# Keys spread by transfers into kept tiles, attention outputs in even rows, and another order of the transfers, in a four-layer conditioned transformer kernel

## The chip, the cores and the metric

The kernel runs on one core of one Trainium2 chip. The metric is the device time of one execution in microseconds. The kernel before was run three times: 1624.05, 1625.13 and 1627.65 us, median 1625.13 us. All arithmetic is float32. In what follows the engines are called PE (matrix multiply; PEld is its weight load), DVE (vector), ACT (activation), POOL (general purpose) and SP (here it only issues transfers); SPq is SP's queue of transfers.

## The reference: what is computed

The input x holds 128 sequences of 64 tokens with 128 channels; there is one conditioning vector for each sequence, and a context of 64 tokens for each. Four layers follow each other, all with residual connections:

- Layer 0: self-attention (normalised x, scaled and shifted by the condition; a gate from the condition on the result), cross-attention to the context, and a gated MLP of 512 hidden units.
- Layer 1: cross-attention to the normalised and modulated context.
- Layer 2: self-attention, cross-attention and MLP like layer 0, with weights of its own.
- Layer 3: attention to the context as a prototype bank, then three routed experts and a gate.

The change touches the attentions of layers 0 to 2, which all have 16 heads of 8 channels:

```python
q = _heads(xn @ q_w + q_b)                       # 16 heads of 8 channels
k, v = (context or xn) @ kv_w + kv_b
attn = softmax(einsum('bhnd,bhsd->bhns', q, k) * SCALE)
o = einsum('bhns,bhsd->bhnd', attn, v)           # back to 128 channels
x = x + gate * (o @ proj_w + proj_b)             # no gate in the cross-attentions
```

## The kernel before

**Tiling and stages.** The 8192 tokens are cut into 16 groups of 512 (8 sequences of 64), and x stays in SBUF in 16 tiles. The program goes through the stages one after the other, each over 16 groups: L0s (self-attention of layer 0), L0c (cross-attention), the MLP of layer 0, L1c, L2s, L2c, the MLP of layer 2, and layer 3. Together the five attention stages are 80 groups.

**Order of the work.** The order on every engine is written out by hand: the program runs under a manual schedule, and each engine takes its instructions in the order of the calls. `attend` is a software pipeline. Its `step(k)` handles a half group (k = 2i + u): the scores of half k, the first half of the exponentials of half k-1, the weighted sums of half k-2, and pieces of two generators, `prepare` for groups up to four ahead and `finish` for groups one to three behind. All transfers are issued by SP in the order of the calls, too. Eight completion semaphores (lanes) are used in turn, so a transfer that is issued waits for the one eight places before it.

**A half group** (`scores`, `turned`, `weighted`): 32 small matmuls give the scores `sc` in PSUM (line 478; the tile has one buffer), DVE takes the maximum `mx` (line 485) and writes the difference `e` (line 487), PE transposes it to `pp` (line 503), ACT takes the exponential `eT` (line 507), PE multiplies it with the values, `po` (line 520), and ACT copies that to `o` (line 528). The weights of the last product, `vbd`, hold the values of a pair of heads and, in two columns, ones, so that the sums of the exponentials (the denominators) come out as further rows of `o`. There are two such tiles, kept for the whole of the attentions; their zeros and ones are written once.

**Keys.** One matmul takes four heads at a time over 32 rows. So the keys of a group, `kT` (line 438, 128 channels by 512 tokens), are spread into `kbd`, which has four copies of it; copy j keeps only the channels of head j of each four, and the rest is zero. Before, POOL makes the four copies by multiplying with a column of 0 and 1 in `mask` (line 444); in the first group of layer 0 DVE does it:

```python
for j in range(4):
    (V if at.get("first") else G).tensor_scalar(
        kbd[:, j], by_batch(kT), mask[:, j : j + 1], 1.0, ALU.mult, ALU.mult
    )
```

**The end of a group** (`finish`, in four pieces). First piece: two transfers bring the rows of denominators of `o` to `sums` in DRAM (line 538), one brings them back as `rc` on 128 partitions (line 542), and four move the odd head pairs' rows of `o` beside the even ones (line 545). Second piece: DVE takes the reciprocal (line 547), a transfer stores it as `recs` (line 549), in the self stages two transfers load the gates `gt` from their table in DRAM (line 278), and one loads the reciprocals back, each repeated over the eight rows of its head, as `rb` (line 554). Third piece: POOL multiplies `o` by `rb` to `oT` (line 557) and adds the bias to x (line 559). Fourth piece: PE projects `oT`, `py` (line 563), and DVE (and in the self stages POOL) adds the result to x (lines 565 to 569).

**The start.** `condition` transposes the condition and the rows of biases; DVE then takes the statistics of the first x tile (line 313), POOL the inverse deviation (lines 329 and 330), DVE normalises (line 372), PE transposes (line 342), DVE modulates (line 357), and PE makes the first keys (line 436).

Of the kernel before, what the change touches and what calls it, by code (L numbers as in the profile page):

```python
# [9 lines left out]
F32 = mybir.dt.float32  # L10
AF = mybir.ActivationFunctionType
ALU = mybir.AluOpType
# [23 lines left out]
for _name, _n in _VECS:  # L36
# [13 lines left out]
    "L3_xcond_router_W": (3, 3), "L3_xcond_e_w1": (9, 256), "L3_xcond_e_w2": (6, 128),  # L50
    "L3_xcond_gate_w1": (3, 128), "L3_xcond_gate_w2": (1, 128), "L3_xcond_out_w": (1, 128),
}
_RAW = [
    "x", "cond_1024", "ctx_1024", *_WTS,
    "L0_xcond_ca_proj_b", "L1_xcond_bp", "L2_xcond_b_cproj", "L3_xcond_router_b", "L3_xcond_e_b2",
# [4 lines left out]
def tile_kernel(ctx: ExitStack, tc: tile.TileContext, a: dict, out: bass.AP):  # L60
# [5 lines left out]
    def const(shape, name):  # L66
        return cp.tile(shape, F32, tag=name, name=name)
# [8 lines left out]
    nc.sync.dma_start(cond, a["cond_1024"])  # L76
    vec_rows = const([_NVEC, P], "vec_rows")
    nc.scalar.dma_start(vec_rows, a["vecs"])
    mask = const([P, 4], "mask")
    nc.scalar.dma_start(mask, a["mask"])  # L80

    w = {}

    def load_weights(prefix, pool=cp):
        for name, (k, n) in _WTS.items():
            if name.startswith(prefix):
                t = pool.tile([P, k, n], F32, tag=name, name=name)
                src = a[name]
                if len(src.shape) == 3:
                    src = src.rearrange("e c n -> (e c) n")  # L90
                nc.sync.dma_start(t, src.rearrange("(k p) n -> p k n", p=P))
                w[name] = t

    xs = [const([P, TT, P], f"x{s}") for s in range(NST)]
# [23 lines left out]

    ident = const([P, P], "ident")
    make_identity(nc, ident)  # L120
    nhalf = const([P, TT], "nhalf")
    G.memset(nhalf, -0.5)

# [37 lines left out]
    def mm(name):  # L161
        return pools[1].tile([P, 512], F32, tag="mm", name=name)
# [4 lines left out]
        Places.ak.tile([P, NB, 8, 32], F32, tag=f"vbd{i}", name=f"vbd{i}", bufs=1) for i in range(2)  # L167
    ]

    def clear(t):  # L170
        G.memset(t, 0.0)
        G.memset(t[0:L, :, :, 16:17], 1.0)
        G.memset(t[L:P, :, :, 17:18], 1.0)


# [2 lines left out]
    condT = const([P, P], "condT")  # L178
    scT = const([P, P], "scT")
    mods = {}  # L180

    def col(name, i=0):
        r = _ROW[name] + i
        return vec[:, r : r + 1]
# [19 lines left out]

    def folded_column(wp, bp, bv, i):
        pb = mm("pb")
        T.matmul(pb[:, 0:1], w[wp][:, 0], col(bv, i), start=True, stop=True)
        t = const([P, 1], "pb_" + wp)
        V.tensor_add(t, pb[:, 0:1], col(bp))
        proj_bias[wp] = t  # L210
# [3 lines left out]
    def gate_table(wmod, wp, i=2, bias=None):  # L214

        table = dp.tile([P, 2, P], F32, tag="gate_" + wp, name="gate_" + wp)
        rows = const([P, 2, P], "gate_rows")
        gb = const([P, P], "gate_bias")
        V.tensor_scalar_mul(gb, mods[wmod][:, i, :], proj_bias[wp] if bias is None else bias)

        def second():
            pg = mm("pg")
            for q, src in enumerate((mods[wmod][:, i, :], gb)):
                T.transpose(pg[:, ts(q, P)], src, ident)
            V.tensor_copy(rows, pg[:, 0 : 2 * P].rearrange("p (i c) -> p i c", i=2))
            nc.sync.dma_start(table, rows)
            gates[wp] = table

        return second

    def folded_row(wp, bp, bv):
        bvs = const([P, P], "bvs")
        V.tensor_copy(bvs, col(bv, 1).broadcast_to([P, P]))

        def second():
            pb = mm("pb")
            T.matmul(pb[:, :P], bvs, w[wp][:, 0], start=True, stop=True)
            V.tensor_add(row_bias[bp], row_bias[bp], pb[:, :P])
            proj_bias[wp] = row_bias[bp]

        return second

    def condition():
        pc = mm("pc")
        T.transpose(pc[:, :P], cond, ident)
        V.tensor_copy(condT, pc[:, :P])
        S.activation(scT, pc[:, :P], AF.Silu)
        pv = mm("pv")
        T.transpose(pv[:, :_NVEC], vec_rows, ident[:_NVEC, :_NVEC])
        V.tensor_copy(vec, pv[:, :_NVEC])  # L250
        V.tensor_scalar_add(vec1, vec, 1.0)

    first_mods = modulations("L0_xcond_adaln_w", "L0_xcond_adaln_b", 6, (1, 4))
# [19 lines left out]
    def gate_tile(pool, s, wp):  # L273

        gt = pool.tile([P, TT, 2, P], F32, tag="gt", name="gt")
        for h in range(2):
            r = gates[wp].rearrange("(s t h) i c -> s h t (i c)", t=TT, h=2)[s, h]
            nc.sync.dma_start(
                gt[ts(h, L)].rearrange("p t i c -> p t (i c)"),
                r.unsqueeze(0).broadcast_to([L, TT, 2 * P]),  # L280
            )
        return gt

# [15 lines left out]
    def by_batch(t):  # L299
        return t.rearrange("p (b l) -> p b l", b=NB)  # L300
# [80 lines left out]

    turn = [0]

    ctxT = dp.tile([NST, P, NT], F32, tag="ctxT", name="ctxT")

    def prepare(pools, at):
# [52 lines left out]
        i = turn[0] % 2  # L439
        turn[0] += 1  # L440
        vbd = vbds[i]
        kbd = pool.tile([P, 4, NB, L], F32, tag="kbd", name="kbd")
        for j in range(4):
            (V if at.get("first") else G).tensor_scalar(  # L444
                kbd[:, j], by_batch(kT), mask[:, j : j + 1], 1.0, ALU.mult, ALU.mult
            )
        yield
        pq = psum.tile([P, 512], F32, tag="mm", name="pq")
        T.matmul(pq, at["wq"], q_in, start=True, stop=True)  # L449
# [11 lines left out]
                    start=True, stop=True,  # L461
                )
        pv4 = pvv.rearrange("p b (i d) -> p b i d", d=HD)
        S.copy(vbd[0:L, :, :, 0:HD], pv4[0:L])
        S.copy(vbd[L:P, :, :, HD : 2 * HD], pv4[L:P])
        at["vbd"] = vbd

    def scores(pools, at, u):
# [61 lines left out]
    def finish(pools, at):  # L530

        pool, psum = pools[:2]
        s, o = at["s"], at["o"]
        cross = at["layer"][2] == "c"

        sums = dp.tile([16, NT], F32, tag="sums", name="sums", bufs=2)
        for j in range(2):
            nc.sync.dma_start(
                sums.rearrange("(g i j) t -> j g i t", i=2, j=2)[j], o[16 + j : P : 32, :, :]
            )  # L540
        rc = pool.tile([P, L], F32, tag="rc", name="rc")
        nc.sync.dma_start(rc, sums.rearrange("h (c t) -> (h c) t", t=L))

        for g in range(4):
            nc.sync.dma_start(o[32 * g + 16 : 32 * g + 32, 0, :], o[32 * g : 32 * g + 16, 1, :])
        yield
        V.reciprocal(rc, rc)
        recs = dp.tile([16, NT], F32, tag="recs", name="recs", bufs=2)
        nc.sync.dma_start(recs.rearrange("h (c t) -> (h c) t", t=L), rc)

        if not cross:
            gt = gate_tile(pool, s, at["wp"])
        rb = pool.tile([P, NT], F32, tag="rb", name="rb", bufs=1)
        nc.sync.dma_start(rb, recs.unsqueeze(1).broadcast_to([16, HD, NT]))
        yield
        oT = pool.tile([P, NT], F32, tag="oT", name="oT", bufs=1)
        G.tensor_tensor(oT, o[:, 0, :], rb, ALU.mult)  # L557
        bias = proj_bias[at["wp"]].unsqueeze(1).broadcast_to([P, TT, P]) if cross else gt[:, :, 1, :]
        G.tensor_tensor(xs[s], xs[s], bias, ALU.add)
        yield  # L560
        py = psum.tile([P, TT, P], F32, tag="mm", name="py")
        for t in range(TT):
            T.matmul(py[:, t, :], oT[:, ts(t, P)], w[at["wp"]][:, 0], start=True, stop=True)  # L563
        if cross:
            V.tensor_add(xs[s], xs[s], py)
        else:
            y = pool.tile([P, TT, P], F32, tag="y", name="y")
            V.tensor_tensor(y, py, gt[:, :, 0, :], ALU.mult)
            G.tensor_tensor(xs[s], xs[s], y, ALU.add)

    def attend(pools, ats):
# [5 lines left out]
        def go(gens, i):  # L577
            if 0 <= i < n:
                next(gens[i], None)
# [8 lines left out]
        def step(k, between=(), late=()):  # L588
# [11 lines left out]
            if past:  # L600
                weighted(pools, past["at"], past["u"], past["eT"])
            if u == 0:
                go(fin, i - 2)
                go(prep, i + 4)
                go(prep, i + 1)
                go(fin, i - 3)
            else:
                go(prep, i + 1)
# [16 lines left out]
    def attention_of(s, layer):  # L625
        if layer[2] == "s":
            wmod, wqkv, bqkv, wp = {
                "L0s": ("L0_xcond_adaln_w", "L0_xcond_qkv_w", "L0_xcond_qkv_b", "L0_xcond_sa_proj_w"),
                "L2s": ("L2_xcond_W_mod", "L2_xcond_W_qkv", "L2_xcond_b_qkv", "L2_xcond_W_proj"),
            }[layer]  # L630
            m = w[wqkv][:, 0]
            return dict(
                s=s, layer=layer, wmod=wmod, wp=wp, wq=m[:, 0:P], bq=col(bqkv, 0),
                wk=m[:, P : 2 * P], bk=col(bqkv, 1), wv=m[:, 2 * P : 3 * P],
            )
        wq, bq, wkv, bkv, wp = {
            "L0c": (
# [8 lines left out]
        }[layer]  # L646
        m = w[wkv][:, 0]
        return dict(
            s=s, layer=layer, wp=wp, wq=w[wq][:, 0], bq=col(bq), wk=m[:, 0:P], bk=col(bkv, 0),
            wv=m[:, P : 2 * P],  # L650
        )

# [537 lines left out]
    def stages():  # L1190
# [41 lines left out]
        clear(vbds[0])  # L1232
        ahead_1(0, 1, 2, 3)
        condition()
        ahead_1(0, 0)
        first_mods[0]()
        ahead_1(0, 0, 1, 2, 0, 0, 1)
# [11 lines left out]
            f()  # L1249
        first_mods[2]()  # L1250
        n = last + 2 + len(heads_0)
        for f in steps_1[6:-n]:
            f()
        for s in range(2):
            heads_0[3 + s] = lambda s=s, f=heads_0[3 + s]: (f(), load_context(s))
        rest = into_mlp(steps_1, heads_0, turns_0)
# [68 lines left out]
```

## Time and profile before

| | |
|---|---|
| runs | 1624.05, 1625.13, 1627.65 us |
| profiled execution | 1626.31 us, span 1624.5 us |
| PE busy | 1573.8 us (97%) |
| DVE busy | 1240.4 us (76%) |
| ACT busy | 1035.5 us (64%) |
| POOL busy | 1072.5 us (66%) |
| `kbd` on POOL | 316 instructions, 212.4 us |
| L0s, first to last start of a group | 16.94 to 204.38 us |
| L0c | 210.47 to 397.72 us |
| L1c | 544.51 to 733.13 us |
| L2s | 739.11 to 925.19 us |
| L2c | 931.28 to 1118.47 us |

The span is one execution as the hardware profiler recorded it; the profiled execution's own time includes what lies around the span. Each attention stage is read at its starts of `mx` for the even halves: a group takes 11.9 to 12.3 us in the steady part. The MLPs and layer 3 fill the time between and after. A "released by" entry in a group of instructions names what ended the idle time before them.

### The profile page before, as it was taken

Reading aid. Unit: us, or ns where it says so; the run is one execution under the profiler, and the core shown is the slowest. Engines: PE = TensorE matmul, PEld = TensorE weight load, DVE = VectorE, ACT = ScalarE, POOL = GpSimd, SP = SyncE. Lnnn points to the kernel's source line nnn. Section 1 sums busy time; section 2 is a strip of 40 time slices with the busy share of each in tenths; the row PEclk is TensorE's granted clock in tenths of the full one; section 3 lists DMA queues with packets and bytes.
Section 4 is the critical chain, followed back from the end, with each engine's and each line's share of the span. In section 5 each row is a group of like instructions: output and inputs, shape, how many; then the busy total and the mean of one; then the engine's idle time right before and its main releaser. Section 6 shows DMA issues by size and latency. Waiting matters only on the chain.

```text
span 1624.5 us, 64028 instructions
## 1 busy us (share of the span) xinstructions
PE 1573.8 (97%) x27842; PEld 1086.8 (67%) x27842; DVE 1240.4 (76%) x1566; ACT 1035.5 (64%) x1710; POOL 1072.5 (66%) x1786
## 2 busy tenths in 40 slices
PE   6999999998999899999999999998999999999998
PEld 4676777776544577776777777776777566666665
DVE  7898998898555688899899889896443566666666
ACT  5788777776433678878888888886334544444443
POOL 6687787766888789887787876775875333333322
PEclk9999999999999999999999999999999999999999
DMA  8334453332111022211334432222533111111100
GB/s 209 85 82 99 107 127 92 83 83 72 55 36 55 16 63 61 72 44 50 90 82 102 104 88 73 62 56 59 130 81 76 31 39 37 40 33 36 34 12 19
DMA packets 146775, 112.65 MB, mean 69 GB/s; under 512 B 36357, under 2 KB 125247, under 8 KB 146495
## 3 DMA queue, kind: packets, MB, share of 16 engines
q1 hardware_dynamic: 146288, 108.53, 26.1%
q8 instruction: 219, 3.59, 0.9%
q14 instruction: 61, 0.50, 0.1%
q10 hardware_dynamic: 207, 0.03, 0.0%
HBM read 83.99 MB, written 14.02 MB: 60 GB/s over the span
## 4 chain that ended last, share of the span: by engine, by line
PE 83%; DVE 12%; ACT 3%; issue 1%; DMA 0%; SPq 0%; DVEq 0%
PE sc L478 10%; PE pp L503 9%; PE po L520 7%; PE ph L693 7%; PE ph L1080 6%; PE ph L1081 6%; DVE e L487 6%; DVE mx L485 6%; PE po L1111 5%; PE psT L342 5%; PE pk L436 5%; PE py L563 4%; PE py L709 4%; PE py L699 3%; PE pvv L459 3%; PE pq L449 3%
## 5 line engine op out<-in xcount | busy, mean ns | idle before, releaser
L507 ACT ACTIVATE eT<-pp 128x1024 f32<-128x1024 f32 x320 | 329.7, 1030 | 160.8 <-PE pp L503 160.7
L485 DVE TENSOR_REDUCE mx<-sc 128x32 f32<-128x2048 f32 x160 | 366.6, 2291 | 83.6 <-PE sc L478 83.6
L487 DVE TENSOR_TENSOR e<-sc,mx 128x2048 f32<-128x2048 f32 x160 | 366.6, 2291 | 5.4
L503 PEld LDWEIGHTS pp<-ident,e 64*128 64x128 f32 x5120 | 183.9, 138 | 140.1 <-ACT eT L507 44.7
L503 PE MATMUL pp<-ident,e 64*128 64x64 f32 x5120 | 227.7, 229 | 7.2 <-DVE e L487 4.7
L444 POOL TENSOR_SCALAR kbd<-kT,mask 128x512 f32<-128x512 f32 x316 | 212.4, 690 | 31.3 <-ACT kT L438 28.3
L372 POOL TENSOR_SCALAR xn<-x,nmu,rs 128x128 f32<-128x128 f32 x508 | 223.6, 453 | 13.3
L557 POOL TENSOR_TENSOR oT<-o,rb 128x512 f32<-128x512 f32 x80 | 102.1, 1276 | 163.5 <-DMA rb<-recs 62.9
L478 PE MATMUL sc<-kbd,qT 32*64 32x256 f32 x5120 | 179.2, 387 | 16.6 <-DVE e L487 15.6
L694 ACT ACTIVATE h<-ph,vec 128x512 f32<-128x512 f32 x128 | 87.3, 687 | 149.9 <-PE ph L693 149.7
L520 PE MATMUL po<-eT,vbd 128*32 128x64 f32 x10240 | 178.1, 221 | 1.4 <-issue 1.3
L1087 ACT ACTIVATE h<-h 128x512 f32<-128x512 f32 x112 | 70.6, 630 | 149.8 <-DVE h L1083 130.9
L520 PEld LDWEIGHTS po<-eT,vbd 128*32 128x32 f32 x10240 | 151.3, 110 | 14.4 <-issue 2.0
L330 POOL TENSOR_TENSOR rs<-rs,nhalf 128x4 f32<-128x4 f32 x128 | 130.2, 1017 | 10.7
L478 PEld LDWEIGHTS sc<-kbd,qT 32*64 32x64 f32 x5120 | 97.7, 131 | 53.0 <-issue 19.6
L1083 DVE TENSOR_TENSOR h<-ph,ab 128x512 f32<-128x512 f32 x112 | 76.9, 687 | 62.6 <-PE ph L1081 62.5
L1116 DVE SCALAR_TENSOR_TENSOR acc<-po,pr,acc 128x128 f32<-128x128 f32 x192 | 67.2, 350 | 44.1 <-PE po L1111 39.6
L1080 PE MATMUL ph<-nx,w 128*128 128x512 f32 x192 | 100.7, 607 | 0.0
L528 ACT COPY o<-po 128x512 f32<-128x512 f32 x160 | 95.7, 598 | 5.1 <-PE po L520 2.0
L1081 PE MATMUL ph<-u,w_ev 128*128 128x512 f32 x192 | 98.9, 597 | 0.0
L1111 PEld LDWEIGHTS po<-w_2o,h 128*128 128x128 f32 x768 | 92.1, 192 | 8.7 <-issue 8.4
L1104 POOL TENSOR_SCALAR g<-g 128x512 f32<-128x512 f32 x16 | 9.9, 622 | 132.1 <-ACT g L1103 132.1
(259 smaller groups left out, 2868.5 us busy)
## 6 DMA issues: line engine op xcount, KB each, us to landing
rb<-recs SPq DMA_DIRECT2D x80, 256.0 KB
c<-in_ctx_dram SPq DMA_DIRECT2D x64, 256.0 KB
o<-o SPq DMA_DIRECT2D x320, 32.0 KB
gt<-gate_L_xcond_sa_proj_w SPq DMA_DIRECT2D x32, 256.0 KB
gt<-gate_L_xcond_W_proj SPq DMA_DIRECT2D x32, 256.0 KB
gt<-gate_L_xcond_W_mlp SPq DMA_DIRECT2D x32, 256.0 KB
x<-in_x_dram SPq DMA_DIRECT2D x16, 256.0 KB
ctxT<-cm SPq DMA_DIRECT2D x16, 256.0 KB
```

The lines of the kernel that those rows point to most:

```text
L330: G.tensor_tensor(rs, rs, nhalf, ALU.pow)
L372: engine.tensor_scalar(xn[:, t, :], src[:, t, :], nmu[:, t : t + 1], rs[:, t : t + 1], ALU.add, ALU.mult)
L444: (V if at.get("first") else G).tensor_scalar(kbd[:, j], by_batch(kT), mask[:, j : j + 1], 1.0, ALU.mult, ALU.mult)
L478: T.matmul(sc[ts(h, L), g, ts(t2, 256)], qT[ts(g, 32), ts(b, L)], kbd[ts(g, 32), :, b, :], start=True, stop=True,)
L485: V.tensor_reduce(mx, sc.rearrange("p g (m k) -> p (g m) k", k=L), AX.X, ALU.max)
L487: V.tensor_tensor(e, sc.rearrange("p g (m k) -> p (g m) k", k=L), mx.unsqueeze(2).broadcast_to([P, 32, L]), ALU.subtract,)
L503: T.transpose(pp[:, h, ts(4 * g2 + 2 * i + t2, L)], e6[ts(h, L), 2 * gg + g2, t2, i], ident[ts(h, L), ts(h, L)],)
L507: S.activation(eT[:, gg], pp, AF.Exp, scale=HD ** -0.5)
L520: T.matmul(po[ts(g, 32), i, ts(2 * t2 + h, L)], at["vbd"][:, 4 * u + 2 * t2 + h, 2 * g + i, :], e7[:, g // 2, h, g % 2, i, t2, :], start=T ...
L1080: T.matmul(ps, wn, d["nx"], start=True, stop=False)
L1081: T.matmul(ps, we, d["u"], start=False, stop=True)
L1111: T.matmul(po[:, ex, :], d[q][:, ts(t, P)], k3["w_2o"][:, q, :], start=r == 0, stop=r == 1)
```

## The change

Six edits belong together.

1. From the third group on, `kbd` is filled by four SBUF-to-SBUF transfers (`spread`) instead of four multiplies. Transfer j copies the rows j, j+4, j+8, ... of `kT` into copy j. There are two kept `kbd` tiles; the first two groups fill them by mask, and the zeros stay.
2. For that, the channels of a block of four heads must lie with the head fastest. The columns of the q and k weights and their biases are reordered at the start: those of layer 0's self-attention by DVE before the first statistics, the others by POOL after half groups of the first stage. The biases get reordered copies (`vecp`, `vecv`), and `mask` is computed instead of loaded.
3. `o` has its data in even rows and the denominators in odd rows: one transfer instead of two for `sums`, and one instead of four for the rows of `o`. The five projection weights are loaded with their rows interleaved to match.
4. In the self stages the gates' loads are issued directly behind `sums`, ahead of `rc`; a partition's piece is one contiguous 4 KB row of the table instead of four of 1 KB.
5. `rb` is loaded in two transfers of 64 partitions directly behind `recs`.
6. In even steps the piece of `prepare` for group i+1 comes ahead of the others, so that `spread` is issued ahead of `recs`; a context load of `prepare` for group i+4 is issued after `rb`.

```diff
+def spread(kbd, kT):
+    for j in range(4):
+        nc.sync.dma_start(kbd[j:P:4, j].rearrange("p b l -> p (b l)"), kT[j:P:4, :])
...
-        kbd = pool.tile([P, 4, NB, L], F32, tag="kbd", name="kbd")
-        for j in range(4):
-            (V if at.get("first") else G).tensor_scalar(
-                kbd[:, j], by_batch(kT), mask[:, j : j + 1], 1.0, ALU.mult, ALU.mult
-            )
+        kbd = kbds[i]
+        by_mask = turn[0] <= 2
+        if by_mask:
+            for j in range(4):
+                (V if at.get("first") else G).tensor_scalar(
+                    kbd[:, j], by_batch(kT), mask[:, j : j + 1], 1.0, ALU.mult, ALU.mult
+                )
+        else:
+            spread(kbd, kT)
...
-        S.copy(vbd[0:L, :, :, 0:HD], pv4[0:L])
-        S.copy(vbd[L:P, :, :, HD : 2 * HD], pv4[L:P])
+        S.copy(vbd[0:L, :, :, 0 : 2 * HD : 2], pv4[0:L])
+        S.copy(vbd[L:P, :, :, 2 * HD : 4 * HD : 2], pv4[L:P])
...
-        for j in range(2):
-            nc.sync.dma_start(
-                sums.rearrange("(g i j) t -> j g i t", i=2, j=2)[j], o[16 + j : P : 32, :, :]
-            )
+        nc.sync.dma_start(sums.rearrange("(m i) t -> m i t", i=2), o[1:P:16, :, :])
+        if not cross:
+            gt = gate_tile(pool, s, at["wp"])
         rc = pool.tile([P, L], F32, tag="rc", name="rc")
         nc.sync.dma_start(rc, sums.rearrange("h (c t) -> (h c) t", t=L))
-        for g in range(4):
-            nc.sync.dma_start(o[32 * g + 16 : 32 * g + 32, 0, :], o[32 * g : 32 * g + 16, 1, :])
+        nc.sync.dma_start(o[1:P:2, 0, :], o[0:P:2, 1, :])
         yield
         V.reciprocal(rc, rc)
...
-        if not cross:
-            gt = gate_tile(pool, s, at["wp"])
         rb = pool.tile([P, NT], F32, tag="rb", name="rb", bufs=1)
-        nc.sync.dma_start(rb, recs.unsqueeze(1).broadcast_to([16, HD, NT]))
+        for i in range(2):
+            r = recs.rearrange("(m i) t -> i m t", i=2)[i]
+            nc.sync.dma_start(rb[i:P:2, :], r.unsqueeze(1).broadcast_to([8, HD, NT]))
...
             if u == 0:
+                go(prep, i + 1)
                 go(fin, i - 2)
                 go(prep, i + 4)
-                go(prep, i + 1)
                 go(fin, i - 3)
...
+def reorder(engine, name, n):
+    for i in range(n):
+        t = const([P, P], "gate_bias")
+        cols = w[name][:, 0, ts(i, P)]
+        engine.tensor_copy(t.rearrange("p (g d j) -> p g d j", d=HD, j=4), by_element(cols))
+        engine.tensor_copy(cols, t)
...
         condition()
+        reorder(V, "L0_xcond_qkv_w", 2)
         ahead_1(0, 0)
...
+            if i % 2 and i // 2 < len(names):
+                reorder(G, *names[i // 2])
```

Beside these, the gate table is stored in two transfers instead of one, in the order that the contiguous load wants.

## The prediction

> **What bounds the kernel now.** I read the page's busy shares, its chain and its groups first, then the list of waits, then the chain and the timeline of one steady stretch, then the timeline of the start.
>
> ```profile
> PE 1573.8 (97%) x27842; PEld 1086.8 (67%) x27842; DVE 1240.4 (76%) x1566; ACT 1035.5 (64%) x1710; POOL 1072.5 (66%) x1786
> ...
> PE 83%; DVE 12%; ACT 3%; issue 1%; DMA 0%; SPq 0%; DVEq 0%
> ...
> L485 DVE TENSOR_REDUCE mx<-sc 128x32 f32<-128x2048 f32 x160 | 366.6, 2291 | 83.6 <-PE sc L478 83.6
> L487 DVE TENSOR_TENSOR e<-sc,mx 128x2048 f32<-128x2048 f32 x160 | 366.6, 2291 | 5.4
> ...
> L444 POOL TENSOR_SCALAR kbd<-kT,mask 128x512 f32<-128x512 f32 x316 | 212.4, 690 | 31.3 <-ACT kT L438 28.3
> L557 POOL TENSOR_TENSOR oT<-o,rb 128x512 f32<-128x512 f32 x80 | 102.1, 1276 | 163.5 <-DMA rb<-recs 62.9 <-PE sc L478 30.3 <-DMA sums<-o 23.0
> ```
>
> PE is busy for 97% of the span and POOL, from which the change takes work, is absent from the chain: 66% busy and never last. The kbd row is what the change removes. The oT row says that POOL's idle time there is a wait for transfers. The chain of 787 to 800 us (start, duration, what) shows the loop of one half group:
>
> ```profile
> 791.56 1.13 PE sc L478 x32
> 792.70 0.02 issue
> 792.72 2.30 DVE mx L485
> 795.02 0.02 issue
> 795.04 2.30 DVE e L487
> 797.35 0.14 issue
> 797.48 1.12 PE sc L478 x32
> ```
>
> sc has one buffer, so scores, maximum and subtraction follow each other: 1.12 + 0.02 + 2.30 + 0.02 + 2.30 + 0.14 = 5.90 us, 11.8 a group; the starts of mx are 11.92 us apart in both self stages and 12.0 to 12.25 in the cross stages. Nothing in this loop is on POOL or the SP queue. They matter where they make DVE (reciprocal) or PE (sc by kbd, py by oT) wait. The waits show how little that is:
>
> ```profile
> POOL oT L557 <- DMA rb<-recs: 62.9, 21, 8.7
> ...
> PEld py L563 <- POOL oT L557: 13.9, 22, 1.6
> ...
> DVE rc L547 <- DMA rc<-sums: 7.5, 2, 3.8
> ```
>
> (us in total, times, longest.) The two reciprocal waits are at ends of attention stages (406 and 1127 us), where mx has already stopped. Profiled time is 1626.31 us, span 1624.5, so 1.8 lie around it; it stands 1.18 above the runs' median 1625.13. I work out differences on the profiled execution and add them to the median.
>
> **kbd by transfers.** Removed: 78 of the 80 groups' four multiplies, 78 x 4 x 690 ns = 215 us at the mean, practically the whole row. In the loop that is worth 0: POOL is not in it, and mx and e take 2291 ns at the mean (2272 to 2293) whether POOL runs beside them or not. Added: 312 transfers of 64 KB. An o<-o issue takes 0.57 to 0.60 us on SP and lands 1.9 after, so four spreads take 4 x 0.62 = 2.5 us of issue and land 3.9 to 4.4 us after kT (5.9 with the straggler of 1.3 that I see when an engine carries a 16 KB instruction packet). From kT's end to the sc that reads kbd are 7.1 us at least (7.3 median): hidden, 0. PE's wait on four lanes in place of POOL stands ahead of its wait for DVE, so it is over when e ends: 0.
>
> **What the spreads push back on SP.** At the place of the timeline below, kT ended at 790.15 and recs was issued 1.74 us later. Now four issues lie between, and recs goes at kT + 2.6: +0.85 us in all groups.
>
> ```profile
> 789.46 0.69 ACT L438 ACTIVATE kT<-pk,vec 128x512 f32<-128x512 f32 x1 [0.40 <-PE pk L436]
> ...
> 790.95 2.69 POOL L444 TENSOR_SCALAR kbd<-kT,mask 128x512 f32<-128x512 f32 x4
> ...
> 791.88 0.33 SPq L549 DMA_DIRECT2D recs<-rc  x1
> ...
> 792.25 1.31 SPq L278 DMA_DIRECT2D gt<-gate_L_xcond_W_proj  x2
> ...
> 793.68 0.54 SPq L554 DMA_DIRECT2D rb<-recs  x1
> ...
> 798.59 1.28 POOL L557 TENSOR_TENSOR oT<-o,rb 128x512 f32<-128x512 f32 x1 [1.71 <-DMA rb<-recs]
> ```
>
> rb is two transfers now: +0.55 for the second issue. Their engines: by the semaphore events a sums transfer (4 outer pieces) posts 5 increments, one at once, where rb (16) posts 16; so pieces decide on how many engines a transfer runs, and halves of 8 pieces should run on 8. rb's 128 packets of 2 KB take 89 ns each, 0.72 us on 16 engines, 1.44 on 8. Bounds: +0.55 (issue alone) to +2.2 (as few as four engines, 2.9 us of packets); I take +0.7.
> The Trainium skill, "DMA: Bandwidth & Descriptors" (section "Why a DMA increments its semaphore by 16 and not by 1"), says that the engines used are the largest number up to 16 dividing the outermost sizes of both sides, the lowest-numbered ones; both halves would then share the same eight. By it the term is +0.7; if halves took different engines it would be +0.55. It speaks against this edit.
>
> Cross stages: rb later by 0.85 + 0.7 = 1.55 us. oT's end to py leaves 2.4 (L0c), 2.8 (L1c), 2.5 us (L2c) at the median; taking the lateness from each of the 48 groups' own slack gives 0.74 + 0 + 0.13 = 0.9 us of PE delay at 1.5 us, 9.2 at 2.2. Taken +0.9, bounds 0 to 9.2.
>
> Self stages: the gates' loads (1.31 us of issue, 512 KB, 2.75 us of packets) no longer stand between recs and rb. From recs' issue to rb's landing were 7.05 us in L0s and 6.83 in L2s, against 5.3 to 5.45 in the cross stages, which have no gt. After: 0.85 + 5.35 + 0.7 = 6.9: the same, 0. By slack, 0.4 later costs 0.4 and 0.75 costs 1.8 in the 32 groups; earlier gains almost nothing, except one stall at 949 us where oT waited 4.5 us for rb and the group took 0.98 longer: -1.0. Bounds -1.4 to +1.8.
>
> **Sums, gates' loads, o.** One sums issue for two (-0.55), one o<-o for four (-1.8 us of SP). gt now sits in SP's wait for the sums, but its packets precede rc's: rc, landing 4.9 to 5.2 us after sums' issue, should land at 5.2 to 6.3. It has 2.1 to 2.5 us in the median before DVE takes it: 0 in the steady groups; in the first, whose gate table landed only at 43.1 us, 0 to 0.8 on DVE, +0.3. In L0c SP works nearly without a pause (sums to sums 11.35 of 12.0 us, with c and ctxT); spreads and a second rb add 3.1 us, sums and o give back 3.4 with their waits, but the order puts sums 1.4 and rc 0.9 us later, below its slack of 2.2: +0.4 (0 to 8, if half a microsecond is lost in 16 groups). Strided vbd writes are ACT copies of the same elements (0.58 us, off the chain): 0. Ten half loads for five projections are issued in the first 6 us or behind the loads of x, long before their use: 0. The POOL reorders (16 copies, about 0.45 us each like xn's 453 ns, 7 us in all, over some ten half groups) go where kbd's 2.7 us a group went: 0.
>
> **The start.** This is the only cost with nothing beside it:
>
> ```profile
> 2.19 0.43 SPq L91 DMA_DIRECT2D L_xcond_qkv_w<-in_L_xcond_qkv_w_dram  x1
> ...
> 4.69 0.76 DVE L313 BATCH_NORM_STATS2 mv<-x 128x6 f32<-128x256 f32 x2 [0.37 <-DMA x<-in_x_dram]
> ...
> 7.16 1.12 DVE L372 TENSOR_SCALAR xn<-x,nmu,rs 128x128 f32<-128x128 f32 x4 [1.71 <-POOL nmu L369]
> ...
> 11.07 2.08 PE L436 MATMUL pk<-xm,L_xcond_qkv_w 128*128 128x512 f32 x2 [2.26 <-DVE xm L357]
> ...
> 16.94 2.29 DVE L485 TENSOR_REDUCE mx<-sc 128x32 f32<-128x2048 f32 x1 [1.36 <-PE sc L478]
> ```
>
> DVE gets four copies of 128 x 128 ahead of the first statistics, and the first of them reads qkv_w, whose transfer was complete at 6.24 us. The copies are like condT's (0.29 us): 6.24 + 4 x 0.3 = 7.5 instead of 4.69: +2.8 us (2.4 to 3.2 with 0.2 to 0.4 a copy). rs, xn, psT, xm, pk, kT, kbd, sc and mx follow in one string, so mx starts at 19.7.
>
> **Sum**: 2.8 + 0.3 + 0.9 + 0 - 1.0 + 0.4 = +3.4: 1625.13 + 3.4 = 1628.5 us.
>
> **Rivals.**
> - Start absorbed (0.20): later groups' work is ready sooner while the first waits, so the first groups (13.31 and 12.78 us against 11.92) shrink. Up to 2.2 us of excess could go: +0.6 to +1.2, about 1626. Against it: those groups contain work of the tables, not waits for x.
> - Faster (0.10): POOL's relief reaches PE. Besides the 13.9 us of py behind oT, PE waited 7.6 for POOL x (L559) and 4.6 for POOL rs. If half of these 26 us vanish: 1628.5 - 13 = 1615.5; it must exceed 6.6 us to give a measurable gain. Against: oT starts 0.16 to 0.19 us after rb lands (medians of four of the five stages), so POOL is not what keeps it.
> - Slower, rb (0.15): it lands 1.5 us later in the self stages too, as spread packets and eight engines add up. The slack gives 7.9 + 5.0 = 12.9 us: 1641.4. It decides from 0.9 us of lateness.
> - Slower, rc (0.10): gt's packets hold rc beyond its slack, and the reciprocal stops DVE inside the loop. From 2.1 us of lateness; 0.5 us in 32 groups are 16: 1644.5.
>
> **Numbers.** The forecast's own case holds 0.45, within 1626.5 to 1631. About 0.2% (3.25 us) is what a measurement tells from no change, so 1628.4 is the line to slower and cuts this case in two. Faster: 0.10 and a little of the absorbed case, 0.11. Same: 0.19 + 0.22 = 0.41. Slower: 0.23 + 0.25 = 0.48. The range takes in rb's case and a small gain, and leaves out rc's and most of the faster one: 1621 to 1642.
>
> **What would show it.** First mx at 19.7 us and L0c's last at the old distance from it; no POOL kbd after two groups, mx and e still 2291 ns; recs 2.6 us behind kT; rb landed 6.0 us behind recs' issue (in all stages); no wait of PE sc for a spread, none of DVE rc for rc within a stage. Wrong if the loop's 5.90 us change, if PE's py wait grows beyond 20 us, or if the start shifts by less than 2 us.

## The result, and the profile after

The changed kernel took 1668.64 us (median of 4 runs, 1667.0 to 1672.91) against 1626.39 us of the kernel before on the same chip: a ratio of 1.0264, 95% interval 1.0238 to 1.0291. It is 42 us slower. The forecast was 1628.5 us with a range of 1621 to 1642, so the sign was right and the size was off by more than ten times.

The page of the changed kernel: busy shares, then the chain that ended last, then three groups.

```profile
PE 1589.0 (95%) x27844; PEld 1090.6 (65%) x27844; DVE 1244.7 (75%) x1575; ACT 1046.5 (63%) x1710; POOL 872.8 (52%) x1490
...
PE 68%; ACT 11%; DMA 9%; DVE 4%; SPq 3%; POOL 3%; issue 2%; POOLq 0%; DVEq 0%; ACTq 0%
...
L551 DVE TENSOR_REDUCE mx<-sc 128x32 f32<-128x2048 f32 x160 | 366.4, 2290 | 90.1 <-PE sc L544 89.8
L553 DVE TENSOR_TENSOR e<-sc,mx 128x2048 f32<-128x2048 f32 x160 | 366.6, 2291 | 5.4
L621 POOL TENSOR_TENSOR oT<-o,rb 128x512 f32<-128x512 f32 x80 | 101.9, 1273 | 346.0 <-DMA c<-in_ctx_dram 104.2
```

POOL lost 200 us of work and nothing became faster for it: mx and e last what they lasted. New in the chain are DMA with 9%, SP's queue with 3% and POOL with 3%, at 0% or absent before; ACT rose from 3% to 11%. POOL's idle time ahead of oT doubled, from 163.5 to 346.0 us. The name behind it ("c") is a transfer that SP issues right behind rb; the multiply reads o and rb, not c. The waits say who pays (us in total, times, longest):

```profile
PEld py L627 <- POOL oT L621: 68.2, 58, 3.2
...
DVE rc L611 <- DMA rc<-sums: 37.0, 29, 2.7
...
PE py L627 <- POOL oT L621: 26.2, 30, 2.4
```

PE waited for oT 58 times instead of 22, and DVE stopped for rc 29 times instead of twice. This table says where the time lies. It goes from a stage's first start of mx to its last one, which is the odd half of the last group (the stage times in the section on the kernel before are read in the same way, though it says even halves):

| from first to last start of mx, us | before | changed | longer |
|---|---|---|---|
| up to the first mx | 16.94 | 20.08 | 3.1 |
| L0s | 187.4 | 196.4 | 9.0 |
| L0c | 187.3 | 200.0 | 12.8 |
| L1c | 188.6 | 192.8 | 4.2 |
| L2s | 186.1 | 195.2 | 9.1 |
| L2c | 187.2 | 194.3 | 7.1 |

The rows add up to 45.3 us. The step into the first MLP was 1.5 us longer too, but what follows L2c was 2.9 shorter: there the kernel before had two stretches of 3.4 us at half clock and the changed one none, beside one at the end of each (last section).

The stages did not become evenly slower. Undisturbed groups of the self stages take 11.87 us (11.92 before) and of L0c 12.01, as before; between them lie groups of 12.3 to 16.2 us. Of the 9.0 us of L0s, 2.1 lie in its first group (15.37 us, 13.31 before), whose keys are made by mask; the last section returns to it. The worst, in L0c, is this piece of the chain (start, duration, what):

```profile
267.98 0.59 SPq L444
268.57 0.04 issue
268.62 0.59 SPq L444
269.21 0.06 issue
269.27 0.02 SPq L613
269.28 0.03 issue
269.31 3.05 DMA recs<-rc
272.36 0.02 issue
272.38 0.02 SPq L618
272.39 0.03 issue
272.42 0.64 SPq L618
273.06 0.05 issue
273.12 0.62 SPq L618
273.74 0.05 issue
273.79 4.11 DMA c<-in_ctx_dram
277.90 0.03 issue
277.93 0.04 POOLq L621
277.97 0.10 issue
278.07 1.27 POOL oT L621
279.34 0.04 issue
279.39 1.16 PE py L627 x8
```

The spreads (L444) stand ahead of recs (L613), recs takes 3.05 us to land, all that time SP stands still, the two halves of rb (L618) go out after it, and oT starts 4.3 us after the second one's issue. PE waited 2.4 us for this py.

The times along that string, as medians of a stage's 16 groups, before and after:

| us | L0s | L0c | L1c | L2s | L2c |
|---|---|---|---|---|---|
| kT's end to recs' issue, before | 1.74 | 1.76 | 1.76 | 1.74 | 1.76 |
| after (predicted 2.6) | 3.2 | 4.3 | 2.5 | 2.9 | 3.1 |
| recs' issue to its landing, before | 1.6 | 1.6 | 1.5 | 1.5 | 1.5 |
| after | 1.7 | 1.7 | 2.5 | 2.8 | 1.8 |
| copy of o to sums' issue, before | 0.0 | 0.9 | 0.0 | 0.0 | 0.0 |
| after | 1.2 | 2.7 | 1.2 | 1.3 | 1.6 |
| rc's landing to the reciprocal, before | 2.1 | 2.2 | 3.0 | 2.5 | 3.0 |
| after | 0.1 | 0.1 | 1.1 | 0.1 | 0.9 |

The last row is the slack on which the prediction counted. In three stages more than half of the groups have none left (the reciprocal starts within 0.1 us of the landing).

### The profile page after: what moved, and what is told of

Its sections match the earlier page's. It is cut to its first block, busy times and chain, and to the rows that moved or that the text cites. A ratio compares the mean times of both kernels' runs of the same rounds, so it can differ in the third digit from the quotient of the medians.

```text
span 1668.2 us, 63910 instructions
## 1 busy us (share of the span) xinstructions
PE 1589.0 (95%) x27844; PEld 1090.6 (65%) x27844; DVE 1244.7 (75%) x1575; ACT 1046.5 (63%) x1710; POOL 872.8 (52%) x1490
## 4 chain that ended last, share of the span: by engine, by line
PE 68%; ACT 11%; DMA 9%; DVE 4%; SPq 3%; POOL 3%; issue 2%; POOLq 0%; DVEq 0%; ACTq 0%
PE pp L569 7%; PE ph L757 6%; PE ph L1144 6%; PE sc L544 6%; PE ph L1145 6%; PE po L1175 5%; PE po L586 5%; ACT eT L573 4%; PE py L627 4%; ACT xm L415 3%; PE py L773 3%; PE psT L398 3%; PE py L763 3%; PE pk L498 3%; PE pq L515 3%; PE pvv L525 3%
## 5 line engine op out<-in xcount | busy, mean ns | idle before, releaser
L553 DVE TENSOR_TENSOR e<-sc,mx 128x2048 f32<-128x2048 f32 x160 | 366.6, 2291 | 5.4
L621 POOL TENSOR_TENSOR oT<-o,rb 128x512 f32<-128x512 f32 x80 | 101.9, 1273 | 346.0 <-DMA c<-in_ctx_dram 104.2
L428 POOL TENSOR_SCALAR xn<-x,nmu,rs 128x128 f32<-128x128 f32 x508 | 225.3, 459 | 13.2
L544 PE MATMUL sc<-kbd,qT 32*64 32x256 f32 x5120 | 183.4, 394 | 13.8 <-DVE e L553 6.7
L386 POOL TENSOR_TENSOR rs<-rs,nhalf 128x4 f32<-128x4 f32 x128 | 130.3, 1018 | 10.6
L544 PEld LDWEIGHTS sc<-kbd,qT 32*64 32x64 f32 x5120 | 99.1, 133 | 52.2 <-issue 15.4
L1175 PE MATMUL po<-w_2o,h 128*128 128x128 f32 x768 | 95.8, 275 | 0.0
L398 PE MATMUL psT<-ident,xn 128*128 128x128 f32 x512 | 82.9, 285 | 3.8 <-DVE xn L428 3.2
```

The costliest lines, as they stand in the source:

```text
L386: G.tensor_tensor(rs, rs, nhalf, ALU.pow)
L398: T.transpose(ps[:, ts(t, P)], src[:, t, :], ident)
L428: engine.tensor_scalar(xn[:, t, :], src[:, t, :], nmu[:, t : t + 1], rs[:, t : t + 1], ALU.add, ALU.mult)
L544: T.matmul(sc[ts(h, L), g, ts(t2, 256)], qT[ts(g, 32), ts(b, L)], kbd[ts(g, 32), :, b, :], start=True, stop=True,)
L553: V.tensor_tensor(e, sc.rearrange("p g (m k) -> p (g m) k", k=L), mx.unsqueeze(2).broadcast_to([P, 32, L]), ALU.subtract,)
L1175: T.matmul(po[:, ex, :], d[q][:, ts(t, P)], k3["w_2o"][:, q, :], start=r == 0, stop=r == 1)
```

## The experiments

Two theories stood against each other at first. Theory SP: SP's queue, with spreads and two waits for landings in one string, has no time left in a group, so each item is issued late and passes its lateness on to the next group. Theory engines: the transfers themselves are slow, because rb's halves run on eight engines and the gates' loads and spreads add bytes. All ratios are to the kernel before, run on the same chip.

**Spreads away.**

```diff
-        by_mask = turn[0] <= 2
+        by_mask = True
```

> The changed kernel, but all 80 groups spread their keys by POOL's four multiplies, so that the 312 spread transfers (2.5 us of issue a group) are gone; everything else stays. Theory SP (the queue of SP has no room for the spreads; sums, rc, recs and rb go out late): nearly all of the 42 us returns but the 3 us of the start, 1627 to 1632 us, and sums goes 0.1 us behind the copy of o again. Theory engines (rb in halves on eight engines, gates' loads ahead of rc): most of the loss stays, 1650 us or more.

Measured: 1633.27 us, ratio 1.0045 (1.003 to 1.006). 35 of the 42 us are the spreads (the time is 1.3 us above theory SP's range). The first mx stayed late (20.66 us), as it must, since the reorders stayed.

**Keys by transfers alone**, in the kernel before, with the order of `prepare`, the reorders, `mask` and the q and k biases of the changed kernel:

```diff
+        kbd = kbds[i]
...
+            spread(kbd, kT)
...
             if u == 0:
+                go(prep, i + 1)
                 go(fin, i - 2)
                 go(prep, i + 4)
-                go(prep, i + 1)
                 go(fin, i - 3)
```

> The kernel before with the keys by transfers alone: spreads ahead of recs, reordered weights and biases; sums in two, o in four, gates' loads behind recs and rb in one transfer as before. Theory SP: SP has more to issue than in the changed kernel (15 transfers a self group against 15 with shorter ones, four of o at 0.6 us each kept), so it is slower than the changed kernel: 1700 us or more, groups above 12.5 us in all stages. Theory engines: without the halves and with rc ahead of the gates' loads it is faster than the changed kernel, 1630 to 1645 us.

Measured: 1711.88 us, ratio 1.0524 (1.0462 to 1.0586); typical groups take 13.3 us in L0s and L0c, and 12.7 to 12.9 in the others. SP issues 15 transfers in such a self group and 12 in the changed kernel, not 15 in both as the expectation has it. So the other edits together (one o transfer for four, one sums for two, gates' loads in the wait, rb in halves) are not what makes the spreads dear; they take half of their cost away. Which of them does is not shown here, and one of them, the gates' loads, costs in the changed kernel (below).

**recs in the middle of the spreads**: the same transfers on the same queue.

```diff
     def spread(kbd, kT):
         for j in range(4):
+            if j == 2:
+                run_between()
             nc.sync.dma_start(kbd[j:P:4, j].rearrange("p b l -> p (b l)"), kT[j:P:4, :])
...
         nc.sync.dma_start(recs.rearrange("h (c t) -> (h c) t", t=L), rc)
 
+        yield
         rb = pool.tile([P, NT], F32, tag="rb", name="rb", bufs=1)
...
             if u == 0:
+                between_spreads[0] = lambda: go(fin, i - 2)
                 go(prep, i + 1)
+                run_between()
                 go(fin, i - 2)
```

`run_between` runs the function that was left for it, once: here the reciprocal and recs of group i-2. The `yield` leaves rb to the call behind.

> The changed kernel with reciprocal and recs issued between the second and the third spread, and rb behind the fourth, so that recs lands while SP issues the last two spreads: the same transfers, but SP no longer stands still for recs' landing. Theory SP: rb is issued 0.8 us earlier, sums of the next group as well; half of the loss or more returns, 1640 to 1652 us. Theory engines: the same transfers on the same engines, 1662 to 1670 us.

Measured: 1633.9 us, ratio 1.0045 (1.0026 to 1.0064), more than theory SP asked for. With all bytes unchanged, 34.7 us return from two spreads' places alone. The cross stages took 186.8, 190.6 and 186.3 us, L2s 185.8; L0s kept 191.5. The timelines of the same half group show how; of their rows only those of SP, the reciprocal and the copy of o are shown. First the changed kernel (start, duration, engine, what):

```profile
796.57 2.40 SPq L444 DMA_DIRECT2D kbd<-kT  x4
797.71 0.54 DVE L611 RECIPROCAL rc<-rc 128x64 f32<-128x64 f32 x1
799.07 0.52 SPq L613 DMA_DIRECT2D recs<-rc  x1
801.55 0.65 ACT L594 COPY o<-po 128x512 f32<-128x512 f32 x1
802.30 1.33 SPq L618 DMA_DIRECT2D rb<-recs  x2
803.73 0.59 SPq L603 DMA_DIRECT2D sums<-o  x1
804.37 2.26 SPq L334 DMA_DIRECT2D gt<-gate_L_xcond_W_proj  x2
...
806.73 0.53 SPq L607 DMA_DIRECT2D rc<-sums  x1
```

Then with recs in the middle:

```profile
776.26 1.12 SPq L453 DMA_DIRECT2D kbd<-kT  x2
777.40 0.54 DVE L620 RECIPROCAL rc<-rc 128x64 f32<-128x64 f32 x1
777.97 0.33 SPq L622 DMA_DIRECT2D recs<-rc  x1
778.34 1.10 SPq L453 DMA_DIRECT2D kbd<-kT  x2
779.55 1.32 SPq L628 DMA_DIRECT2D rb<-recs  x2
781.24 0.64 ACT L603 COPY o<-po 128x512 f32<-128x512 f32 x1
781.90 0.59 SPq L612 DMA_DIRECT2D sums<-o  x1
```

In the first, the reciprocal was done at 798.25, but recs went at 799.07, behind the spreads, and rb only 3.2 us later; the copy of o ended at 802.20 and sums had to wait 1.5 us. In the second, recs goes as soon as the reciprocal is done, the last two spreads fill its landing, rb follows 1.6 us behind recs, and sums follows the copy at once. It is so in most groups: recs went 0.03 us behind the reciprocal in the kernel before (median of each stage), 0.8 to 1.3 in the changed one, and 0.03 again here.

Theory SP says more than that, namely that a round of SP has no time left. That holds for a part of the rounds: in the changed kernel SP came to the first spread later than kT (by more than 0.12 us) in 26 of 78 groups, ten of them in L0c, and in the others it stood waiting for kT. With the keys alone it was late in 68 of 78, with recs in the middle in 2.

**Gates' loads back between recs and rb**, in the changed kernel:

```diff
         nc.sync.dma_start(sums.rearrange("(m i) t -> m i t", i=2), o[1:P:16, :, :])
-        if not cross:
-            gt = gate_tile(pool, s, at["wp"])
         rc = pool.tile([P, L], F32, tag="rc", name="rc")
...
+        if not cross:
+            gt = gate_tile(pool, s, at["wp"])
         rb = pool.tile([P, NT], F32, tag="rb", name="rb", bufs=1)
```

> The changed kernel with the gates' loads again between recs and rb in the self stages, all else as changed. If the gates' loads ahead of rc cost the self stages their 18 us (rc landing late, DVE waiting for it): L0s and L2s come back to within 5 us of before, 1652 to 1658 us. Theory SP: 1.3 us of issue only moves from the wait for sums into the string recs, rb, sums, which is full: self stages grow further, 1670 to 1690 us. The cross stages change by less than 3 us either way.

Measured: 1659.74 us, ratio 1.0208 (1.0179 to 1.0238): 9 us better than the changed kernel. L0s went from 196.4 to 193.3 and L2s from 195.2 to 189.1, so this part of theory SP fell: loads that precede rc do cost, once rc has no slack. The other theory promised a little too much: L0s stayed 5.9 us above before, and the time is 1.7 above its range. The bound of 3 us for the cross stages failed as well (L0c +4.1, L2c -5.2); lateness comes and goes in single groups there.

**The gates' loads' place alone, in the kernel before** (with the contiguous rows of the table):

```diff
+        if not cross:
+            gt = gate_tile(pool, s, at["wp"])
         rc = pool.tile([P, L], F32, tag="rc", name="rc")
...
-        if not cross:
-            gt = gate_tile(pool, s, at["wp"])
         rb = pool.tile([P, NT], F32, tag="rb", name="rb", bufs=1)
```

> The kernel before with one part of the change alone: the gates' loads directly behind sums, ahead of rc, with contiguous 4 KB rows. In the self stages rb no longer waits behind 512 KB, 1.3 us sooner, but rc does. From the slacks: 0.98 us at one stall and little else to gain, rc 0.5 to 1 us later within a slack of 2: 1624.5 to 1627, no measurable difference. Rival (rc stops DVE): L0s and L2s 2 to 6 us longer, 1629 to 1636.

Measured: 1626.23 us, ratio 0.9997 (0.9985 to 1.0009). Here rc lands about 1.5 us later before its reciprocal too, not 0.5 to 1 (slack 0.6 in L0s and 0.9 in L2s instead of 2.1 and 2.5), and the whole time does not change. L0s was 2.3 us longer, 2.0 of it in the first group (last section), L2s 1.4 shorter. The same edit is free here and costs 9 us in the changed kernel, where sums is already late.

**rb in two halves, alone, in the kernel before:**

```diff
-        nc.sync.dma_start(rb, recs.unsqueeze(1).broadcast_to([16, HD, NT]))
+        for i in range(2):
+            nc.sync.dma_start(
+                rb[ts(i, L), :], recs[ts(i, 8), :].unsqueeze(1).broadcast_to([8, HD, NT])
+            )
```

> The kernel before with rb alone cut into two transfers of eight source rows each (64 partitions each). Theory halves (eight engines and a second issue make rb land later, which the ends of stages and the groups with little slack feel): rb lands 0.6 to 0.8 us later behind its issue, the last L0c group to the first hidden matmul of the MLP grows, and the time rises by 3 to 6 us, 1630 to 1633. Rival (what remains in the changed kernel without spreads is due to the start and to layout, not to rb): within 1 us of before.

Measured: 1632.17 us, ratio 1.0038 (1.0024 to 1.0052). rb landed 4.4 to 4.7 us behind its first issue in the cross stages, 3.4 to 3.5 before: 0.9 to 1.3 later, not 0.6 to 0.8.

**The rest of the change without the keys** (old column order and biases, mask loaded):

```diff
-        by_mask = turn[0] <= 2
+        by_mask = True
...
-        reorder(V, "L0_xcond_qkv_w", 2)
...
-                reorder(G, *names[i // 2])
```

> The changed kernel without its keys: POOL's multiplies in all groups, weights and biases in their old column order, mask loaded, no reorders; o in even rows, one sums and one o transfer, gates' loads ahead of rc and rb in halves stay. Theory halves: 1627 to 1631, the first maximum back at 17 us, the step into the first MLP still 1.4 us longer. Rival (shorter transfers of sums and o pay): 1620 to 1625.

Measured: 1630.95 us, ratio 1.0025 (1.0014 to 1.0036), with the first mx at 16.81 us. Shorter sums and o transfers gain nothing that shows; the halves cost what they cost alone.

**Eight engines or sixteen.** recs is stored twice, so that each half of rb has sixteen source rows; once without the keys and once with them, recs in the middle and a late reorder.

```diff
-        recs = dp.tile([16, NT], F32, tag="recs", name="recs", bufs=2)
-        nc.sync.dma_start(recs.rearrange("h (c t) -> (h c) t", t=L), rc)
+        recs = dp.tile([32, NT], F32, tag="recs", name="recs", bufs=2)
+        for q in range(2):
+            nc.sync.dma_start(
+                recs.rearrange("(m q i) (c t) -> q m (i c) t", q=2, i=2, t=L)[q], rc
+            )
...
-            nc.sync.dma_start(rb[i:P:2, :], r.unsqueeze(1).broadcast_to([8, HD, NT]))
+            nc.sync.dma_start(rb[i:P:2, :], r.unsqueeze(1).broadcast_to([16, 4, NT]))
```

> The changed kernel without its keys by transfers and without reorders (o in even rows, one sums and one o transfer, gates' loads ahead of rc), with recs stored twice so that each half of rb has sixteen source rows. Theory eight engines: of the 5 us that this kernel lost with eight rows most returns, 1626 to 1628. If it is the second issue and the order of the gates' loads: 1629 to 1632.

> As the run with recs in the middle and the late reorder, but recs is stored twice (two transfers of 32 KB, +0.35 us on SP), so that each half of rb has sixteen source rows instead of eight. Theory eight engines: rb lands 0.5 to 0.7 us sooner behind its first issue, less the 0.35, and the step into the first MLP shrinks by about 0.5 us: 1629 to 1631. Rival (two issues, not the engines, are what makes rb late): landing within 0.2 us of the run with eight rows, time equal or 1 to 3 us longer.

Measured: 1631.17 us, ratio 1.0034 (1.0017 to 1.005), and 1636.38 us, ratio 1.0064 (1.0042 to 1.0085). The engines are as supposed: in the trace each half of eight rows posts 9 semaphore increments and each half of sixteen posts 16, and rb lands 3.3 to 3.8 us behind its first issue in the cross stages, with eight rows 4.1 to 4.4. But the time did not return. So eight engines explain rb's landing behind its own issue. Whether they also cost the last 5 us these runs cannot say, because the second store took back what they gained: recs landed 2.6 to 2.7 us behind its first issue instead of 1.4 to 1.8, and from recs' issue to rb's landing the cross stages took 6.0 to 6.8 us with sixteen rows and 5.7 to 6.3 with eight. The engines, the second issue and the order of SP's string are left, and no run here separates them.

**The start**: recs in the middle, and the reorder behind the statistics.

```diff
         condition()
-        reorder(V, "L0_xcond_qkv_w", 2)
         ahead_1(0, 0)
+        reorder(V, "L0_xcond_qkv_w", 2)
```

> The changed kernel with recs between the spreads (as in the run before with recs in the middle) and, added, the reorder of the first q and k weights behind the first statistics instead of ahead of them. If the start is a plain string as predicted: first maximum at 17.3 to 17.8 us instead of 19.95, and 2.2 to 2.8 us less in all, 1631. If the time is taken elsewhere in the start, the first maximum stays above 19.

Measured: 1633.25 us, ratio 1.0039 (1.0023 to 1.0054): the whole time did not fall (1633.9 before the edit). The first mx came at 18.76 us, 1.2 sooner, not 2.2 to 2.8. The first sc started at 16.65 us instead of 18.74, 2.1 sooner; but it took 2.01 us here and 1.12 there. The string is as predicted, except that the copies now stand between DVE's normalisation and its first modulation values, where they still cost 0.9 (first sc at 15.72 us in the kernel before).

**The spreads on other queues**, with the changed kernel's order; ACT's, and in a second kernel POOL's (`nc.gpsimd`):

```diff
-            nc.sync.dma_start(kbd[j:P:4, j].rearrange("p b l -> p (b l)"), kT[j:P:4, :])
+            nc.scalar.dma_start(kbd[j:P:4, j].rearrange("p b l -> p (b l)"), kT[j:P:4, :])
```

> The changed kernel with the 312 spreads issued by ACT behind its own kT instead of by SP: same transfers, same bytes, SP free of 2.5 us a group. Theory SP: the cross stages, where ACT has 9.1 us of work a group and 2.4 more fit into 12, come back to 187 to 191 us each; in the self stages ACT has 10.3 us and 12.7 with the issues, more than the loop's 11.9, so those grow by up to 0.8 us a group, 196 to 200 us each; in all 1645 to 1660. Theory of bytes (the spreads' packets hold up the others): the cross stages stay at 193 to 200 us.

> The changed kernel with the spreads issued by POOL in the place of its multiplies. No run here shows what such an issue costs on POOL. Theory SP: if it is less than the 690 ns of a multiply, all stages come back to those of the changed kernel without transfers, 1631 to 1637; if it is 1.5 us or more, POOL's string to oT gets longer than before and the stages stay above 190 us, 1645 or more. Theory of bytes: 1655 or more in either case.

Measured: on ACT 1762.24 us, ratio 1.0837 (1.081 to 1.0864); on POOL 1637.45 us, ratio 1.0077 (1.0052 to 1.0102). POOL's issues take 0.54 us at the median, less than a multiply, and all stages return to 185.3 to 190.7 us (185.4 to 190.8 with the spreads away): the same bytes, off SP's string, cost nothing there. The time on POOL's queue is 0.5 us above the range of theory SP. On ACT the sum of work was the wrong measure. An ACT line of that run, with what ended its wait:

```profile
1007.53 2.41 ACTq L444 DMA_DIRECT2D kbd<-kT  x4
...
1009.99 1.02 ACT L573 ACTIVATE eT<-pp 128x1024 f32<-128x1024 f32 x1 [2.49 <-DMA kbd<-kT]
```

The exponential, due every 2.95 us, stands behind four issues of 2.4 us in all (the row names their transfer; what it waits for is ACT's own issuing, over at 1009.94), and PE behind the exponential (the weight loads of pp waited 182 us for eT, 43 in the changed kernel): 13.2 to 13.9 us a group in every stage, cross stages included.

## Why the prediction was wrong, step by step

- **The bound and POOL's relief**: right. mx and e stayed at 2291 ns, no stage gained from 200 us less work on POOL, and the groups that nothing disturbs kept their length (within 0.05 us).
- **The spreads hidden from sc**: right in itself; no wait of PE for a kbd transfer is among the larger ones, and the loss came over another way.
- **"+0.85 us in all groups" for what the spreads push back: the step that failed.** It put the spreads into one round of SP, with everything ahead of them on time, and asked only whether that round's rb came within oT's slack. Measured were recs 2.5 to 4.3 us behind kT and its landing up to 1.4 us longer behind the spreads. From kT's end to rb's landing the cross stages took 2.4 to 3.3 us longer than before (medians; 1.55 predicted), the self stages 0.8 and 2.1 (0 predicted). And SP issues sums behind rb: sums went 1.2 to 2.7 us behind the copy of o, and rc with it, a delay that the forecast counts in L0c alone. Where rc has no slack left, DVE stops for it, and in a third of the groups SP was still late at the next spreads. The cross stages, +0.9 and +0.4 in the forecast, took 24.1 us more. Its two slower rivals, rb late (1641) and rc late (1644), were priced one at a time; both hang on recs in the same string of SP and came together. Moving recs between the spreads showed it: 34.7 us back with the same transfers.
- **Self stages 0**: wrong by 9 us each, for this reason, but for the 2.1 us in the first group of L0s, which came without any spread (+0.3 predicted). rc landed 6.7 and 6.2 us behind sums (5.2 to 6.3 predicted), 1.5 and 1.3 later than before, and sums itself went 1.2 and 1.3 later; together 2.7 and 2.6 us against the slacks of 2.1 and 2.5 that the forecast relied on.
- **rb in halves +0.7, by eight engines**: right in kind. The Trainium skill, "DMA: Bandwidth & Descriptors" (section "Why a DMA increments its semaphore by 16 and not by 1"), gives the number of engines by the outermost sizes, and the trace agrees: 9 increments for eight rows, one at once and eight as data land, 16 for sixteen. The size was 0.9 to 1.3 us of landing, and alone it cost about 6 us of time (1632.17 against 1626.04) where the forecast had it as part of 0.9.
- **The start +2.8**: the sum was close, 3.1 measured, the parts were not. qkv_w was complete at 5.93 us and the copies took 1.1, so the statistics started 2.27 later; another 0.89 came from the first sc, which took 2.01 us instead of 1.12; the reorder does not decide that (last section). Over the profiles with this reorder in place the first sc started at 17.9 to 18.7 us, without it at 15.4 to 16.1: 1.9 to 3.4, which holds the 2.8. The rival that the start is absorbed got nothing: L0s did not shrink.
- **The stall at 949 us, -1.0**: cannot be seen under the new ones. The term itself was right: in the kernel before with the gates' loads' place alone, the stall is gone, and the group that took 12.99 us takes 12.00.

The first copy and the first statistics of the changed kernel's start, to be held against the prediction's rows (the statistics at 4.69 us):

```profile
5.93 0.28 DVE L283 COPY gate_bias<-L_xcond_qkv_w 128x128 f32<-128x128 f32 x1 [1.28 <-DMA L_xcond_qkv_w<-in_L_xcond_qkv_w_dram]
...
6.96 0.75 DVE L369 BATCH_NORM_STATS2 mv<-x 128x6 f32<-128x256 f32 x2
```

Together: about 35 us for the order of the spreads on SP, 3 for the start (0.9 of it in the first sc), some 5 that rb's halves alone also cost. No variant was measurably faster than the kernel before.

## What to carry to other kernels

A queue that issues in order and waits for landings is a resource with a length of its own: add up a round of it, issues and standstills, and compare it with the period, because it does not show up as busy time of any engine. It can cost before it is full: here SP stood waiting for the keys in two thirds of the rounds and was late behind them. Put work that can be issued at once into the queue's waits (two spreads into the landing of recs) and nothing between a result that is ready and the short transfer which carries it on. A slack taken from a trace holds for the sum of all delays ahead of it, not for each alone; and where the end of one round starts the next, the rounds have to be followed until they settle.

## What the runs showed of the hardware that had not been expected

A stall of PE can cost more than its length. These are the windows around the stall at 277 us of the changed kernel: the window, its length, the busy time of PE, PEld, DVE, ACT and POOL, then PEclk (the granted share of the clock), the busy share of the DMA engines and GB/s.

```profile
272.00:279.00 7.00, 4.92 (x136) 3.17 (x130) 6.33 (x5) 4.62 (x7) 0.93 (x1) 1.00 0.38 119
279.00:281.00 2.00, 1.61 (x20) 1.49 (x22) 0.10 (x1) 0.00 (x0) 1.83 (x4) 0.93 0.18 58
281.00:284.00 3.00, 3.00 (x46) 1.83 (x42) 1.00 (x2) 1.61 (x2) 2.87 (x6) 0.50 0.33 114
284.00:288.00 4.00, 4.00 (x118) 2.74 (x112) 3.49 (x2) 2.47 (x4) 0.00 (x0) 0.98 0.29 88
```

After PE had waited 2.4 us its clock was granted at half from 280.7 us on, for 3.4 us, and the scores in it took 1.86 us instead of 1.12: the group took 16.19 us instead of 12.01, 4.2 lost and not 2.4. The clock records list such stretches of 3.4 us (or twice that): three in the kernel before, 10.6 us in all, six in the changed one, 24.2 us, eleven in the one with the keys alone, 41.2 us. At half speed that is at most 7 of the 42 us. The Trainium skill, "TensorE: Matmul & The Clock Gate" (Part 1, on the clock gate), has the array's clock halved after an idle window of about 3.4 us that runs freely. The lengths agree with these records, but the window was not idle: in the 3.4 us ahead of each of the changed kernel's stretches, the one at its end aside, PE was busy for 1.0 to 1.5 us, and the wait at 277 us was 2.4 us long. Not each stall has a stretch behind it: py waited 58 times for oT, and the attention stages of that profile hold four.

One of the four lies at 31.6 us, in the first group of L0s, which took 15.37 us. In all 14 profiles together, that group takes 14.9 to 15.4 us in the nine that have such a stretch between 27 and 36 us, and 13.3 to 13.8 in the five that have none, the kernel before among them; rb's halves alone are without it and the gates' loads alone have it. So about 2 us of a difference in L0s come and go with it.

The first sc of an execution takes either 1.12 or 2.01 us:

```profile
15.72 1.12 PE L478 MATMUL sc<-kbd,qT 32*64 32x256 f32 x32 [0.87 <-DVE kbd L444]
...
17.98 2.01 PE L544 MATMUL sc<-kbd,qT 32*64 32x256 f32 x32 [0.87 <-DVE kbd L508]
```

The first row is of the kernel before, the second of the changed one. It took 2.01 us in eight of the fourteen profiles, two of them of kernels without any reorder (rb in halves alone, gates' loads alone), and 1.12 in the six others, three of them with one. The clock records tell the two apart: in the six, the first record of a fully granted clock begins ahead of the first sc (at 13.8 to 17.1 us, 15.1 in the kernel before), in the eight only after it (at 18.9 to 22.2 us, 21.3 in the changed kernel). So 0.9 us of a difference between two profiles can come from there, and no run tells what sets the time of the first record.
